# Pooled outputs of the 5x5 layer sent through DRAM and fetched back by quarters of the image

## The chip, the core and the metric

The kernel runs on one core of one Trainium2 chip. A core has TensorE (PE, matmuls, with its weight loads as PEld), VectorE (DVE), ScalarE (ACT), GpSimd (POOL) and SyncE (SP, which issues DMAs here); each takes its instructions in order, and they meet through semaphores. The metric is the device time of one execution in microseconds, the median of several runs. Less is better.

## The reference, cut to what matters

The input is 16 images of 32 channels of 128x128. Four layers follow each other, each with a group normalisation ahead of it and a residual sum behind it:

```
x = x + L0(gn(x))     a recurrent layer, 128 steps with gates
x = x + L1(gn(x))     an "adder" 3x3 layer: out = -sum |patch - w|
x = x + L2(gn(x))     a Hartley transform, 32x32 modes mixed, and back
x = x + L3(gn(x))     five edge operators, normalised, then a small U-net
```

The change lies in L3. Its first steps are

```
y = concat of five normalised 3x3 edge operators of x      (160 channels)
y = maxpool2(conv3x3(y, conv1_w) + conv1_b)                128x128 -> 64x64
y = maxpool2(conv3x3(y, conv2_w) + conv2_b)                64x64 -> 32x32
...                                                        down to 16x16 and back up
out = x * y
```

The kernel folds the edge operators, their normalisation and conv1 into one 5x5 layer of 32 input and 32 output channels, whose weights depend on the statistics of the image. As adding a constant commutes with a maximum, the bias of conv1 is added after the pooling.

## The kernel before, in words

**The stages.** stage0 computes L0. Then `rest` computes L1 with the class Differences: 16 images, two halves each, so 32 units; each unit makes 72 tiles of 128 x 64 rows x 128 or 130 columns in fp16, of |x - w| in its one-sided form, on either ScalarE (L705, `d_act`) or VectorE (L708, `d_dve`), and TensorE sums them (L595). L2 and L3 are computed by the class After for groups of four images (g = 0 to 3), 32 channels of four images filling the 128 partitions.

**The order.** All instructions are written out in one order (`keep_order` then fixes it for every engine). A planner, the class Weave, keeps planned times for PE, DVE and ACT. For each tile Differences picks the engine that would end first, at planned prices of 2.36 us for VectorE and 7.15 us for ScalarE, and between tiles `advance` lets the generator of After emit work for as long as PE has room. After's code adds its own planned prices to `weave.dve` and `weave.act`, so that the share-out of the tiles follows. `weave.later(us, step)` puts a step off by so many planned microseconds, and `weave.done(step)` runs one now if it has not run yet. Groups 0, 1 and 2 are taken one after the other beside Differences; when Differences ends, `drain` interleaves what is left of group 2 with group 3, which needs the last image; `weave.alone` is set when group 2 is done.

**The 5x5 layer** (`conv1`, L1612). The image is cut in 8 chunks of 16 rows. For each chunk, 25 taps x 16 matmuls (L1671) fill four PSUM banks, one for each image `blk` of the group. In a bank the 128 partitions are (j, o): row block j of four rows, output channel o. VectorE corrects the two border columns (L1707) and takes the 2x2 maximum into the tile `pooled` (L1595), 128 partitions of 2 rows x 64. The next layer wants another layout: tile `y1`, with partition (blk, channel) and a padded image of 66x66 in the free dimension. The helper `spread` (L1599) moves the data there: for every blk and every j it copies 32 partitions to their place and adds the bias `b1[:, blk]` on the way, on ScalarE (L1609) or, when `weave.alone` is set and blk is even, on VectorE (L1606). That is 16 small copies a chunk, put off by 5 planned us. The last chunk's `spread` is kept as `self.rest_of_y1`.

**Before and after it.** The frames of input rows come by L1307 and are normalised on ScalarE (L1313, L1319, L1320). conv2 (L1518) reads y1 in two passes of 32 rows; ahead of the second pass, `rest_of_y1` is run (L1511).

**Other transfers on SyncE.** Each unit of Differences loads its quantised image half, 2.1 MB in fp16 (`loaded`, L562, `q<-q_d`), emitted at tile 8 of the unit before; `xq` loads (L539) and their stores (L555) prepare the next image. All are issued from SyncE.

Of the kernel before, what the change touches and what calls it, by code (L numbers as in the profile page):

```python
# [7 lines left out]
F32 = mybir.dt.float32  # L8
# [897 lines left out]
class After:  # L906
# [547 lines left out]
    def first_layers(self, g, fp, frames, y2):  # L1454
        nc, tc, weave = self.nc, self.tc, self.weave
        sides = fp.tile([128, H + 4, 4], F32, name="sides")
        ops = fp.tile([128, 2, 5], F32, name="ops")
        wf = fp.tile([128, 90, 32], F32, name="wf")
        b1 = fp.tile([128, 4], F32, name="b1")
        with self.pool("e_v", self.buffers["e_v"]) as pool:  # L1460
            v = []

            def table():

                k, half = len(v) // 2, len(v) % 2
                v.append(pool.tile([128, 45, 32], F32, name="v"))
                nc.gpsimd.dma_start(
                    v[-1].rearrange("p t o -> p (t o)"), self.d["fold"][k, :, 1440 * half : 1440 * half + 1440]
                )

            with self.pool("e_s") as es:
                yield from self.statistics(g, es, frames, sides, ops, lambda: [table() for _ in range(self.buffers["e_v"])])
            yield -0.5
            for n in range(10):
                k, half = n // 2, n % 2
                for part, i in (((0, 81 - 45), 0), ((81 - 45, 45), 1)) if half else (((0, 45), 0),):
                    s = ops[:, i, k : k + 1]
                    to, t = wf[:, 45 * half + part[0] : 45 * half + part[1]], v[n][:, part[0] : part[1]]
                    if k == 0:
                        nc.vector.tensor_scalar(to, t, s, None, ALU.mult)  # L1480
                    else:
                        nc.vector.scalar_tensor_tensor(to, t, s, to, ALU.mult, ALU.add)
                    weave.dve += 0.1 + 0.033 * (part[1] - part[0])
                if len(v) < 10:
                    table()
                yield -2.0
        with self.pool("e_y1") as y1p:
            y1 = self.padded(y1p, 64, "y1")
            self.wc = {"conv2": replicated(nc, y1p, self.a["conv2"], 9, "w_conv2")}
            yield from self.conv1(g, y1p, frames, y1, sides, wf, b1)  # L1490
            with self.pool("e_c2") as cp:
                yield from self.small_layers(cp, None, y1, y2)

    def small_layers(self, cp, rp, y1, y2):
# [11 lines left out]
        def conv(src, n, name, evict):  # L1506
            rows = min(n // 4, 512 // n)
            for r in range(0, n, 4 * rows):
                acc = [self.acc() for _ in range(4)]
                if r:  # L1510
                    weave.done(self.rest_of_y1)  # L1511
                for tap in range(9):
                    kh, kw = tap // 3, tap % 3
                    for j in range(4):
                        for blk in range(4):
                            part = slice(32 * blk, 32 * blk + 32)
                            at = r + rows * j + kh
                            nc.tensor.matmul(  # L1518
                                acc[blk][32 * j : 32 * j + 32, : rows * n],
                                wc[name][part, tap, :],  # L1520
                                src[part, at : at + rows, kw : kw + n],
                                start=tap == 0,
                                stop=tap == 8,
                            )
                    yield rows * n / 512 * 1.0 + 0.15
                yield SUMMED
                for blk in range(4):
                    evict(r, rows, acc[blk][:, : rows * n], blk)
                yield -2.0
# [82 lines left out]
    def conv1(self, g, pool, frames, y1, sides, wf, b1):  # L1612
# [10 lines left out]
        ahead = self.buffers["frames"]  # L1623
        ready = {(n // 2, n % 2): normalise(n // 2, n % 2, 4.0 + 3.0 * n) for n in range(2 * ahead)}
        p = self.acc()
        for j in range(4):
            nc.tensor.matmul(p[32 * j : 32 * j + 32, :4], tap_of("all", 25), cst["m4_bc"], start=True, stop=True)
        yield SUMMED
        nc.vector.tensor_scalar(b1, p[:, :4], self.bias[:, 0:1], None, ALU.add)


        cps = [self.acc() for _ in range(4)]
# [22 lines left out]
            nc.vector.tensor_copy(cut[:, blk].rearrange("p s h r -> p (s h r)"), cps[blk][:, :64])  # L1655
        weave.dve += 0.8

        spreads = []
        for ch in range(H // R):
            xp = chunk(ch)  # L1660
            yield ("done", ready[ch, 0])
# [37 lines left out]
            if ch + ahead < H // R:  # L1699
                for half in range(2):  # L1700
                    load(ch + ahead, half)
                    ready[ch + ahead, half] = normalise(ch + ahead, half, 26.0 + 4.0 * half)
            out = []
            for blk in range(4):
                a4 = acc[blk].rearrange("p (r w) -> p r w", w=W)
                for s, col in enumerate((0, W - 1)):
                    nc.vector.tensor_tensor(a4[:, :, col], a4[:, :, col], cut[:, blk, s, ch, :], ALU.add)  # L1707
                weave.dve += 0.3
                out.append(self.pooled(pool, acc[blk], 4, W))

            def spread(top=1 + R // 2 * ch, out=out):
                for blk in range(4):
                    self.spread(
                        lambda part, j: y1[part, top + 2 * j : top + 2 * j + 2, 1:65],
                        out[blk],
                        blk,
                        b1[:, blk : blk + 1],
                        nc.scalar,
                    )

            spreads.append(weave.later(5.0, spread))
            yield -2.0
        self.rest_of_y1 = spreads.pop()
        for v in spreads:
            weave.done(v)

    def last(self, g):

# [213 lines left out]
def program(nc, tc, a, at, out):  # L1942
    def scratch(name, *shape):
        return nc.dram_tensor(name, shape, F32, kind="Internal").ap()

    d = {f"x{i}": scratch(f"x{i}_d", B, C, H, W) for i in (1, 2, 3)}
    d["q"] = nc.dram_tensor("q_d", (B, C, H + 2, W + 2), F16, kind="Internal").ap()
    d["xm"], d["z"] = (scratch(n, B, C, M1, M1) for n in ("xm_d", "z_d"))
    d["y6"] = scratch("y6_d", NG, 128, 66 * 66)
    d["fold"] = scratch("fold_d", 5, 128, 90 * 32)  # L1950
    d["up"] = scratch("up_d", 3, 128, 25 * 32)
    with tc.tile_pool(name="keep", bufs=1) as keep:
        cw = keep.tile(list(a["consts"].shape), F32, name="cw")
        nc.scalar.dma_start(cw, a["consts"])
        cst = {n: cw[:, lo:hi] for n, (lo, hi) in at.items()}
        sel16 = keep.tile([128, 9, 32], F16, name="sel16")
        nc.scalar.dma_start(sel16, a["sel16"])
        bias = keep.tile([128, 10], F32, name="bias")
        nc.scalar.dma_start(bias, a["bias"])

        m1, r1 = stage0(nc, tc, keep, cst, a["x"], a["xs"], a["w0"], a["b1"], a["b2"], d["x1"])
        rest(nc, tc, cst, sel16, bias, m1, r1, a, d, out)
# [17 lines left out]
```

## Time and profile before

| what | value |
|---|---|
| time, median of 3 runs (lowest, highest) | 7199.5 us (7186.45, 7207.52) |
| span of the profiled execution | 7206.6 us |
| busy: PE, DVE, ACT | 5631, 5845, 5498 us |
| d_act tiles on ScalarE, d_dve tiles on VectorE | 631 of 7.143 us, 1673 of 2.362 us |
| copies y<-pooled,b on ScalarE (L1609) | 488, 195.0 us, 0.400 us each |
| 5x5 layer runs (L1671): groups 0 and 1 | about 2824 to 3340 and 4470 to 4960 us, beside the adder layer |
| 5x5 layer runs: groups 2 and 3 | about 6180 to 6510 and 6680 to 7013 us, after it |
| adder layer ends | about 5945 us |
| data moved by DMA | 722.57 MB |

A line of a group gives code line, engine, operation, what is written and read, shapes and count, then busy time and mean duration, then idle time ahead of these instructions and what ended it. In a timeline, the bracket at the end of a line gives the idle time ahead of it and its releaser.

### The profile page before, as it was taken

What the parts mean: (1) busy time and instruction counts of PE and PEld (TensorE: products, weight loads), DVE (VectorE), ACT (ScalarE), POOL (GpSimd) and SP (SyncE); (2) the same over time, 40 slices, a digit from 0 to 9 for tenths busy, and PEclk for the clock granted to TensorE, in tenths of its full rate; (3) what the DMA queues carried; (4) which work ended last, traced back from release to release, by engine and by line L of the source; (5) the groups of instructions that cost most, each with busy time, mean ns of one, the idle gap of its engine ahead of it and who ended that gap; (6) DMA issues with size and microseconds to landing.
All of it is one profiled execution on the core that took longest, in us unless ns stands there. A gap on an engine that the chain in (4) does not pass through costs nothing. (4 is left out here: it accounts for less than half of the span.)

```text
span 7206.6 us, 271424 instructions
## 1 busy us (share of the span) xinstructions
PE 5631.0 (78%) x127740; PEld 3001.3 (42%) x127740; DVE 5845.3 (81%) x7099; ACT 5498.0 (76%) x3100; POOL 111.8 (2%) x91
## 2 busy tenths in 40 slices
PE   4778567777877777998777787999776784797896
PEld 3665333333334343333334343333333443554564
DVE  7787689999998989999998999999998994134224
ACT  2555489999998989999999999999998991131222
POOL 0000000000000000000000001000000000000000
PEclk9899789999988898999888998999888986798997
DMA  8664211111133432221343343221252245252324
GB/s 310 230 205 144 83 63 57 55 58 47 47 101 93 141 98 81 63 69 47 78 126 98 115 118 104 65 65 46 57 134 92 64 136 150 89 170 74 86 51 98
DMA packets 372719, 722.57 MB, mean 100 GB/s; under 512 B 50896, under 2 KB 217296, under 8 KB 360720
## 3 DMA queue, kind: packets, MB, share of 16 engines
q1 hardware_dynamic: 364128, 670.79, 30.6%
q0 software_dynamic: 7040, 33.80, 1.4%
q8 instruction: 999, 16.37, 1.0%
q14 instruction: 120, 0.98, 0.0%
q10 hardware_dynamic: 432, 0.64, 0.0%
HBM read 507.28 MB, written 164.32 MB: 93 GB/s over the span
## 5 line engine op out<-in xcount | busy, mean ns | idle before, releaser
L705 ACT ACTIVATE d_act<-q,neg 128x8192 f16<-128x8192 f16 (+1 forms) x631 | 4462.6, 7143 | 184.4 <-PE acc L595 135.0
L708 DVE TENSOR_SCALAR d_dve<-q,qw 128x8192 f16<-128x8192 f16 (+1 forms) x1673 | 3859.4, 2362 | 200.8 <-PE acc L595 158.0
L595 PE MATMUL acc<-d_dve,sel 128*32 128x512 f16 x26768 | 1869.8, 402 | 504.0 <-DVE d_dve L708 454.0
L595 PEld LDWEIGHTS <-sel 128*32 128x32 f16 x36864 | 1026.9, 100 | 2164.4 <-issue 1507.8
L1671 PE MATMUL acc<-xp,wf 32*32 32x512 f32 x25600 | 1043.7, 618 | 37.6 <-issue 32.8
L595 PE MATMUL acc<-d_act,sel 128*32 128x512 f16 x10096 | 724.4, 408 | 356.2 <-ACT d_act L705 343.6
L1671 PEld LDWEIGHTS acc<-xp,wf 32*32 32x32 f32 x25600 | 431.9, 104 | 416.5 <-issue 329.6
L625 PE MATMUL acc<-q,zero 128*32 128x512 f16 x7248 | 522.9, 401 | 0.0
L1609 ACT ACTIVATE y<-pooled,b 32x128 f32<-32x128 f32 x488 | 195.0, 400 | 414.4 <-DVE pooled L1595 407.8
L207 PE MATMUL pg<-h,wb 64*64 64x20 f32 (+15 forms) x4096 | 395.7, 320 | 106.1 <-DVE h L256 64.8
L852 PE MATMUL acc<-y,u_conv 32*32 32x256 f32 (+1 forms) x9728 | 359.8, 459 | 76.0 <-issue 46.6
L244 ACT ACTIVATE gt<-pg,bias 128x20 f32<-128x20 f32 (+15 forms) x1024 | 315.8, 374 | 80.2 <-PE pg L207 73.1
L1313 ACT ACTIVATE xp<-xp,shift,stats 128x1280 f32<-128x1280 f32 (+1 forms) x128 | 182.6, 1434 | 240.5 <-DMA xp<-x_d 210.1
L207 PE MATMUL pg<-e,wb 64*64 64x20 f32 (+15 forms) x4096 | 353.1, 315 | 16.4 <-DVE e L260 5.4
L207 PEld LDWEIGHTS pg<-h,wb 64*64 64x64 f32 x4096 | 248.3, 154 | 140.7 <-DVE h L256 90.4
L625 PEld LDWEIGHTS <-zero 128*32 128x32 f16 x7248 | 218.6, 102 | 203.0 <-issue 46.1
L207 PE MATMUL pg<-xn,wb 64*64 64x28 f32 (+61 forms) x4096 | 284.5, 302 | 11.3 <-ACT gt L244 3.8
L207 PEld LDWEIGHTS pg<-e,wb 64*64 64x64 f32 x4096 | 251.5, 156 | 92.1 <-DVE e L260 62.9
L1354 PE MATMUL acc<-xp 32*64 32x204 f32 (+3 forms) x8576 | 238.5, 344 | 37.8 <-ACT xp L1319 28.8
L1800 DVE TENSOR_SCALAR s<-acc,l_ms,l_one 128x512 f32<-128x512 f32 x128 | 102.3, 824 | 199.0 <-PE acc L852 199.0
L255 ACT ACTIVATE th<-c 128x20 f32<-128x20 f32 (+15 forms) x256 | 81.3, 320 | 235.5 <-DVE c L253 234.1
L852 PEld LDWEIGHTS acc<-y,u_conv 32*32 32x32 f32 x9728 | 171.4, 110 | 196.6 <-issue 130.4
(215 smaller groups left out, 4303.1 us busy)
## 6 DMA issues: line engine op xcount, KB each, us to landing
xr<-x_d SPq DMA_DIRECT2D x192, 512.0 KB
xp<-x_d SPq DMA_DIRECT2D x112, 640.0 KB
q<-q_d SPq DMA_DIRECT2D x32, 2145.0 KB
x_d<-xr SPq DMA_DIRECT2D x128, 512.0 KB
x_in<-in_x_dram SPq DMA_DIRECT2D x16, 2048.0 KB
res<-in_x_dram SPq DMA_DIRECT2D x64, 512.0 KB
xn<-in_xs_dram SPq DMA_DIRECT2D x64, 512.0 KB
xn<-xn SPq DMA_DIRECT2D x128, 256.0 KB
```

The source lines that it names most:

```text
L207: nc.tensor.matmul(bank[c][q][64 * pair : 64 * pair + 64, :, :width], wb[half, 4 * kind + KIND[q]].rearrange("p b o -> p (b o)"), v[half], ...
L244: nc.scalar.activation(gt[:, q, :, :n], bank[c][q][:, :, :n], AF.Tanh if q == G else AF.Sigmoid, bias=bias[:, KIND[q] : KIND[q] + 1],)
L595: self.nc.tensor.matmul(acc[k][32 * j : 32 * j + 32, :], self.sel16[:, i // 9, :], d[:, row : row + 4, c : c + W], start=first, stop=last,)
L625: self.nc.tensor.matmul(acc[k][32 * j : 32 * j + 32, :], self.zero, q[:, :4, :W], start=False, stop=False)
L705: nc.scalar.activation(dst, src, AF.Relu, bias=self.neg[:, i : i + 1])
L708: nc.vector.tensor_scalar(dst, src, self.qw[:, i : i + 1], 0.0, ALU.subtract, ALU.max)
L852: nc.tensor.matmul(acc[blk][32 * j : 32 * j + 32, o : o + rows * n], t[part, 4 * par + tap, :], src[part, top : top + rows, left : left + ...
L1313: nc.scalar.activation(v, v, AF.Identity, bias=self.shift3, scale=self.stats3[:, 1])
L1354: nc.tensor.matmul(gram[blk][j : j + width, at : at + n], xp[part, l, 2 + j : 2 + j + width], xp[part, rows, j : j + width + 4], start=sta ...
L1609: nc.scalar.activation(d, s, AF.Identity, bias=bj)
L1671: nc.tensor.matmul(acc[blk][32 * j : 32 * j + 32, :], tap_of("all", tap)[rows], xp[rows, 4 * j + kh : 4 * j + kh + 4, kw : kw + W], start= ...
L1800: nc.vector.tensor_scalar(s.rearrange("p r w b -> p b r w"), acc[blk].rearrange("p (b r w) -> p b r w", b=2, w=64), istd[:, blk : blk + 1] ...
```

## The change

The pooled outputs no longer go straight from tile to tile. VectorE writes the four maxima of a chunk into one tile `po`, and four DMAs store it at once to a DRAM buffer `y1_d`, in the layout (image, channel, pixel). At chunks 2, 4 and 6 a fetch of 16 pooled rows (two earlier chunks) into y1 is put off by 12 planned us; after the last chunk two fetches of 8 rows follow, put off by 6 and 8. With each fetch comes a step `biased`, 12 planned us later (6 for the last two), in which one ScalarE operation adds the bias in place over all 128 partitions. The bias tile therefore becomes one column over (blk, o). Before conv2 starts, the first four pieces are completed, and ahead of its second pass the last. The planner is told 0.25 + 0.054 us a row for `biased`, where it was told 0.45 us for each copy. The change is for having one ScalarE operation a quarter where there were 16 a chunk.

```diff
-        b1 = fp.tile([128, 4], F32, name="b1")
+        b1 = fp.tile([128, 1], F32, name="b1")
...
                 if r:
-                    weave.done(self.rest_of_y1)
+                    self.rest_of_y1()
...
-        for j in range(4):
-            nc.tensor.matmul(p[32 * j : 32 * j + 32, :4], tap_of("all", 25), cst["m4_bc"], start=True, stop=True)
+        for blk in range(4):
+            nc.tensor.matmul(
+                p[32 * blk : 32 * blk + 32, :1], tap_of("all", 25), cst["m4_bc"][:, blk : blk + 1], start=True, stop=True
+            )
...
-        nc.vector.tensor_scalar(b1, p[:, :4], self.bias[:, 0:1], None, ALU.add)
+        nc.vector.tensor_scalar(b1, p[:, :1], self.bias[:, 0:1], None, ALU.add)
...
-        spreads = []
+        y1_d = self.d["y1"][g]
+
+        def store(ch, po):
+            for blk in range(4):
+                to = y1_d[blk][:, 512 * ch : 512 * ch + 512]
+                first = to.offset
+                nc.sync.dma_start(
+                    bass.AP(to.tensor, first, [[128, 4], [4096, 32], [1, 128]]), po[:, blk]
+                )
+
+        coming = {}
+
+        def fetch(top, rows, after):
+            nc.sync.dma_start(
+                y1[:, 1 + top : 1 + top + rows, 1:65],
+                y1_d.rearrange("b o (r w) -> (b o) r w", w=64)[:, top : top + rows],
+            )
+            coming[top] = weave.later(after, lambda: biased(top, rows))
+
+        def biased(top, rows):
+            v = y1[:, 1 + top : 1 + top + rows, 1:65]
+            nc.scalar.activation(v, v, AF.Identity, bias=b1[:, 0:1])
+            weave.act += 0.25 + 0.054 * rows
+            coming[top] = None
+
+        def complete(top):
+            while coming.get(top):
+                weave.done(coming[top])
+
...
-            out = []
+            po = pool.tile([128, 4, 128], F32, name="po", bufs=2)
...
-                out.append(self.pooled(pool, acc[blk], 4, W))
-
-            def spread(top=1 + R // 2 * ch, out=out):
-                for blk in range(4):
-                    self.spread(
-                        lambda part, j: y1[part, top + 2 * j : top + 2 * j + 2, 1:65],
-                        out[blk],
-                        blk,
-                        b1[:, blk : blk + 1],
-                        nc.scalar,
-                    )
-
-            spreads.append(weave.later(5.0, spread))
+                src = acc[blk].rearrange("p (r a w b) -> p r w a b", a=2, b=2, w=W // 2)
+                nc.vector.tensor_reduce(po[:, blk].rearrange("p (r w) -> p r w", w=W // 2), src, AX.XY, ALU.max)
+                weave.dve += 0.65
+            store(ch, po)
+            if ch in (2, 4, 6):
+                top = 8 * ch - 16
+                coming[top] = weave.later(12.0, lambda top=top: fetch(top, 16, 12.0))
             yield -2.0
-        self.rest_of_y1 = spreads.pop()
-        for v in spreads:
-            weave.done(v)
+        coming[48] = weave.later(6.0, lambda: fetch(48, 8, 6.0))
+        coming[56] = weave.later(8.0, lambda: fetch(56, 8, 6.0))
+        for top in (0, 16, 32, 48):
+            complete(top)
+        self.rest_of_y1 = lambda: complete(56)
```

More of the change, by code (lines that the diff above doesn't have):

```diff
@@ L1948, in program @@
     d["xm"], d["z"] = (scratch(n, B, C, M1, M1) for n in ("xm_d", "z_d"))
+    d["y1"] = scratch("y1_d", NG, 4, 32, 64 * 64)
     d["y6"] = scratch("y6_d", NG, 128, 66 * 66)
```

## The prediction, made before the result was known

> **What bounds the kernel now.** I first read the page's forty slices (180 us each), to see which stages there are.
>
> ```profile
> PE   4778567777877777998777787999776784797896
> ...
> DVE  7787689999998989999998999999998994134224
> ACT  2555489999998989999999999999998991131222
> ```
>
> From slice 6 to slice 33 (900 to 5945 us) VectorE and ScalarE are both at 9 or close to it: this is the adder layer, 32 units of 72 tiles, which the two engines share out (5030 us, so 157 us a unit). After it comes a tail of 1260 us in which both are nearly idle and PE is high. Next I asked for the busy time in stretches (columns: PE, weight load, DVE, ACT, POOL, clock, DMA share, GB/s): one slice of the adder layer without the 5x5 layer, two in which the 5x5 layer (L1671) of groups 0 and 1 runs under it, then the tail in four stretches.
>
> ```profile
> 1260.00:1440.00 180.00, 137.18 (x2328) 64.26 (x2324) 177.57 (x199) 172.08 (x27) 0.00 (x0) 0.94 0.15 56
> 2880.00:3060.00 180.00, 171.92 (x3836) 64.22 (x3828) 169.51 (x112) 178.27 (x89) 0.00 (x0) 0.98 0.21 63
> 4680.00:4860.00 180.00, 178.57 (x3999) 67.36 (x3984) 173.00 (x119) 175.96 (x96) 4.68 (x1) 0.99 0.22 66
> ```
> ```profile
> 5945.00:6180.00 235.00, 105.80 (x2830) 85.93 (x2817) 98.15 (x232) 23.33 (x41) 9.06 (x14) 0.63 0.50 150
> 6180.00:6680.00 500.00, 427.44 (x13194) 246.08 (x13195) 169.11 (x454) 117.65 (x248) 8.58 (x18) 0.89 0.35 104
> 6680.00:7013.00 333.00, 302.52 (x9523) 205.00 (x9521) 80.08 (x175) 76.22 (x145) 0.21 (x1) 0.95 0.31 71
> 7013.00:7206.60 193.60, 126.09 (x4408) 84.89 (x4386) 82.81 (x171) 48.37 (x80) 0.00 (x0) 0.77 0.44 98
> ```
>
> Under the adder layer the 5x5 layer makes three engines full at once: ScalarE 178 and 176 of 180, PE 172 and 179, VectorE 170 and 173. In the tail the 5x5 layer of group 2 (6180 to 6510) and of group 3 (6680 to 7013) run on PE, with ScalarE at a quarter. So a ScalarE microsecond counts under groups 0 and 1 and is free under 2 and 3. The groups between 2880 and 3240 us show what this ScalarE time is made of (count, busy us, mean ns, idle before):
>
> ```profile
> L705 ACT ACTIVATE d_act<-q,neg 128x8192 f16<-128x8192 f16 (+1 forms) x42 | 297.9, 7146 | 1.9 <-PE acc L595 1.7
> ...
> L1609 ACT ACTIVATE y<-pooled,b 32x128 f32<-32x128 f32 x96 | 38.3, 399 | 1.3
> ...
> L543 ACT ACTIVATE xq<-xq,shift,r 128x1024 f32<-128x1024 f32 x4 | 4.9, 1232 | 1.6 <-DMA xq<-x_d 1.6
> ```
>
> The 96 small bias copies take 38 us of 360 and wait for almost nothing; a copy of 128x1024 takes 1.23 us. Last I looked for what a late transfer does in this layer, in the timelines of SyncE, ScalarE and VectorE around 2550 to 2605 us:
>
> ```profile
> 2549.65 0.56 SPq L562 DMA_DIRECT2D q<-q_d  x1
> 2557.11 37.98 SPq L1307 DMA_DIRECT2D xp<-x_d  x3
> ```
> ```profile
> 2596.48 1.46 ACT L1313 ACTIVATE xp<-xp,shift,stats 128x1280 f32<-128x1280 f32 x1 [23.29 <-DMA xp<-x_d]
> ```
> ```profile
> 2601.86 2.35 DVE L708 TENSOR_SCALAR d_dve<-q,qw 128x8192 f16<-128x8192 f16 x1 [17.79 <-PE acc L595]
> ```
>
> A frame load queued behind the 2.1 MB load of q came late, ScalarE stood 23.3 us, and PE and VectorE followed: 17.8 us lost by all. A transfer that ScalarE waits for in its in-order queue is no private matter of ScalarE.
>
> **What the Trainium skill says.** (1) "DMA: Bandwidth & Descriptors", section "Why a DMA increments its semaphore by 16 and not by 1": a transfer is spread over the largest number of engines up to 16 that divides the slowest dimension of both sides. The load of q starts with a broadcast dimension of 4, hence 4 engines; the trace agrees, with a DMA share of 0.25 to 0.28 for some 35 us after its issue at 4490.7. The new stores also start with a dimension of 4, and the fetches with 128. (2) Same page, "Queues, rings and completion order": each engine takes one issuer's descriptors in ring order. So a fetch on 16 engines has a quarter of its pieces behind a running q load; the two waits above agree, and so does the xq load issued at 3030.5, for which ScalarE waited until 3071. (3) Same page, "Anatomy of one DMA — SWDGE (gpsimd) path": about 2 us fixed, most of it the receipt of the write. That is told of the other issue path; the chain here shows a 640 KB frame load at 4.7 us. (4) Same page, "Why small descriptors are slow (HBM only)": 256-byte pieces cost 27% more; the fetches' rows are 64 x 4 = 256 bytes. No row of before shows that.
>
> **The change, part by part.**
> Removed from ScalarE, per group: 8 chunks x 16 copies x 0.400 = 51.2 us. Added: three of 16 rows (128x1024, 1.23 us) and two of 8 rows (128x512, not shown; on the line between 0.40 at 128 elements and 1.23 at 1024 it is 0.76): 5.2 us. Net 46 us a group, 92 us in the two groups under the adder layer. There the planner gives x tiles from VectorE (2.36 us each) to ScalarE (7.14): 2.36x = 92 - 7.14x, x = 9.7, and both end **23 us** earlier. The planner's own prices (0.45 a copy, 0.25 + 0.054 a row) free 105.8 us, 11.1 tiles, 26 us. I take 23, bounds 15 and 27.
>
> Unchanged: eight border additions and four reductions a chunk on VectorE; the four matmuls of the bias (one column for four). The 32 stores and 5 fetches a group take SyncE about 0.5 us each (L555, 0.54 us), 20 us a group, on a queue with some 20 issues in 360 us: nothing. The stores wait for the four reductions, some 4 us after the chunk's last matmul; queued behind them are frame, xq and q loads issued 10 us and more ahead of their use: nothing to 2 us. Traffic: 4 MB a group on 722 MB.
>
> Added wait: a ScalarE bias op for each fetch, planned 12 us after it (6 for the last two). A fetch lands in about 6 us (4.7 us for 640 KB, 512 KB with the 27%, and its issue); behind q it takes up to 40 (3030.5 to 3071). The slack is 12 us plus half a tile of ScalarE queue, 16, less 6: 10 us. The q load fills 35 of 157 us, so of ten fetches under the adder layer about 2 fall into it, and such a one is on average (35-10)^2/(2 x 35) = 9 us too late. Of that the buffers hide some 5 (23.3 against 17.8). Expected **5 to 8 us**, bounds 0 and 40; I take 5.
>
> Moved: PE. With 46 us of ScalarE free, 6.4 more tiles are made while one group's 5x5 layer runs, each about 1.1 us of PE (L595: 232 us for 224 tiles, and L610), and PE was full: 7 us, and the tiles made in those 7 us again, 7/(1-0.54) = 15 us a group. So at the end of the adder layer, 23 us sooner, group 2 stands 23 + 30 = 53 us further back. Its missing work there (end of the Hartley back transform, 7 us an iteration that holds 1.3 us of PE) shrinks to about 25 us once nothing paces it; and in the tail it then waited for transfers anyway (ScalarE 25.6, 11.2 and 14.9 us for frames between 5940 and 5996). PE fills only from 6180. I take **5 us** of lengthening, bounds 0 and 25.
>
> The junction to conv2 in the tail: the 5x5 layer ended at 7012.9, conv2's first pass ran at once until 7023.4, the last copy began at 7018.2. Now: reductions until 7017, store 2 to 3 us, fetch 4 to 6, bias 0.8: 7024 to 7027. The second pass waits 1 to 4 us; I take **2**. In group 2 ScalarE stands in this wait with group 3's frames behind it: 0 to 5, counted in the 5 above.
>
> Sum: 7199.5 - 23 + 5 + 5 + 2 = 7188 (7188.5).
>
> **Rivals.**
> (B) Full gain: no fetch meets a q load, and group 2's delay vanishes in the transfers of 5945 to 6180, where PE is 45% busy: 7199.5 - 26 - 4 (less contention on ScalarE in the tail) = 7170. For it: those transfer waits; against it: two frame or xq loads did meet q in before.
> (C) The gain is paid back: two late fetches at 9 and the whole 7 us of (A)'s rest: 7199.5 - 23 + 18 + 7 = 7202, no change. For it: ScalarE's 23 us stall that carried VectorE along.
> (D) Slower: the late fetches hit the quarter before conv2, where PE itself stands in its in-order queue, so with two full hits at 18 us and group 2's 25 us, 7199.5 - 23 + 36 + 25 = 7238. For it: in before the q load of 3318 would still run when the last eighth of group 0 is stored (after 3337); PE is full from 6180, so lateness of group 2 can come through whole. Against it: both bounds at once.
>
> **How the numbers follow.** A 0.42 (7188, give or take 15: 0.13 faster by over 0.3%, that is below 7178; 0.26 within; 0.03 slower). B 0.23 (0.22 faster, 0.01 within). C 0.14 (0.09 within, 0.05 slower, above 7221). D 0.21 (slower). Together faster 0.35, same 0.36, slower 0.29. The range 7150 to 7240 leaves out the outer half of D and the best of B. The planner lays the whole order anew, and no row of before shows how its chunks fall against the q loads; that is the greatest unknown.
>
> **What would show it.** Right: ScalarE's copies y<-pooled,b gone, ten bias ops of about 1.2 and 0.8 us under the adder layer; L705's count up by about 10 and L708's down by as many; the adder layer's last d_dve near 5922 instead of 5944; the tail 1262 to 1275 us. Wrong: ScalarE idle behind a DMA into y1 by more than 15 us in all, with VectorE idle on PE of like length; the first L1671 of group 2 more than 260 us after the adder layer's end; PE idle ahead of conv2 (L1518) by over 5 us in group 3. The forecast fails upwards if fetches are late more than twice, downwards if the tail shortens too.

## The result, and the profile after

The changed kernel takes 7370.5 us (median of 4 runs, 7358.3 to 7371.8) against 7202.3 us for the kernel before (7186.5 to 7207.5): a ratio of 1.0235, interval 1.0219 to 1.0250. It is 168 us slower, above the forecast range.

The loss has two seats. The adder layer ends at 6016 us instead of 5941.5 (+75), and the tail behind it lasts 1354 us instead of 1265 (+88). The page's forty slices of the changed kernel, now 184 us each:

```profile
PE   4788477778777778887776776988877776599986
...
DVE  7787599999989989887998998988999892512334
ACT  2556399999989999888998999988999860120101
```

ScalarE and VectorE fall to 8, in one slice to 7, in slices 17 to 19 and 27 to 28, counted from 1, while the 5x5 layer (now L1701) of groups 0 and 1 runs: the stretches where both were full. The same stretches in numbers, as shown for before, then the tail in four parts (columns: PE, weight load, DVE, ACT, POOL, clock, DMA share, GB/s):

```profile
1260.00:1440.00 180.00, 137.14 (x2348) 64.54 (x2344) 177.57 (x200) 173.27 (x27) 0.00 (x0) 0.95 0.15 55
2880.00:3060.00 180.00, 167.30 (x3648) 62.72 (x3618) 167.94 (x112) 158.47 (x35) 0.00 (x0) 0.96 0.25 67
4680.00:4860.00 180.00, 170.60 (x3852) 65.37 (x3841) 173.00 (x111) 174.99 (x40) 0.00 (x0) 0.98 0.21 65
```
```profile
6016.00:6430.00 414.00, 249.19 (x5612) 200.37 (x5611) 199.86 (x470) 48.44 (x89) 18.08 (x31) 0.61 0.66 207
6430.00:6700.00 270.00, 241.90 (x7285) 141.83 (x7284) 65.19 (x174) 48.82 (x82) 2.59 (x6) 0.91 0.31 86
6700.00:7112.00 412.00, 373.01 (x12276) 268.26 (x12276) 104.09 (x294) 46.04 (x63) 0.42 (x2) 0.97 0.25 58
7112.00:7369.00 257.00, 174.72 (x5658) 107.39 (x5654) 113.33 (x225) 39.19 (x41) 0.00 (x0) 0.76 0.48 106
```

The stretch at 1260 is as before. At 2880, ScalarE has 35 instructions instead of 89, is 20 us less busy, and PE lost 4.6 us with it: the relief is there, and time is lost beside it. In the tail, the stretch up to group 2's 5x5 layer (PE busy 249 of 414 us, clock 0.61) is longer: the layer's first L1701 starts 420 us after the adder layer's end. In before the first L1671 of group 2 starts at 6204.8 us, 263 us after the end, and not at 6180, where the stretches above the prediction put it.

What holds ScalarE in the adder layer is said by its waits (us in total, times, longest), in before from 2700 us to 5941 us and in after from 2700 us to 6016 us:

```profile
ACT d_act L705 <- PE acc L595: 109.0, 26, 14.3
ACT xp L1313 <- DMA xp<-x_d: 1.9, 1, 1.9
```
```profile
ACT y L1681 <- DMA y<-y_d: 136.6, 7, 28.5
ACT d_act L705 <- PE acc L595: 104.6, 27, 19.7
ACT xp L1313 <- DMA xp<-x_d: 23.2, 3, 18.3
```

The bias operation (L1681) stands 136.6 us behind its fetch, in 7 waits for its ten fetches. Five waits, of 21 to 29 us, belong to the six large fetches (16 rows) and make 123 us of the sum. The other two, of 8.3 and 5.2 us, come at the end of each group's layer, where the last stores, a fetch of 8 rows and its bias follow each other directly. The first of the five, in the timelines of SyncE, ScalarE and VectorE:

```profile
3027.26 2.40 SPq L1666 DMA_DIRECT2D y_d<-po  x3
3029.76 0.65 SPq L562 DMA_DIRECT2D q<-q_d  x1
3030.46 0.83 SPq L1673 DMA_DIRECT2D y<-y_d  x1
```
```profile
3064.78 1.15 ACT L1681 ACTIVATE y<-y,b 128x1024 f32<-128x1024 f32 x1 [24.15 <-DMA y<-y_d]
3065.84 1.45 ACT L1313 ACTIVATE xp<-xp,shift,stats 128x1280 f32<-128x1280 f32 x1
```
```profile
3079.99 4.62 DVE L708 TENSOR_SCALAR d_dve<-q,qw 128x8192 f16<-128x8192 f16 x2 [22.11 <-PE acc L595]
```

The fetch is issued 0.7 us after the load of q and lands some 34 us later; ScalarE stands 24 us, and VectorE stands 22 us until 3080, because PE had waited 22.7 us for ScalarE's tile. It is the picture shown for a frame load of before, but it repeats. In group 0 the loads of q are issued at 3029.8, 3180.8 and 3344.4 us and the fetches at 3030.5, 3182.7 and 3348.9; in group 1 two of three again follow within 3 us (4869.5 and 4871.3; 5033.3 and 5035.8), and the third fetch leaves 8 us ahead of its load (5188.3 and 5196.4) and isn't waited for. Five of six is hard to put down to chance. A fetch comes every second chunk, and group 0's 5x5 layer now holds 285 tiles, so 285/4 = 71 tiles from fetch to fetch; a load of q comes every 72 tiles. The two periods are nearly equal, so one meeting is followed by the next. With the 251 tiles of before it would be 63 tiles, and in e6 below, which has that share-out, two of six follow a load of q directly. This reading rests on issue times; no run varied the period alone.

The share-out moved, but little of it the way it was meant to (first two lines of before, then of after):

```profile
L705 ACT ACTIVATE d_act<-q,neg 128x8192 f16<-128x8192 f16 (+1 forms) x631 | 4462.6, 7143 | 184.4 <-PE acc L595 135.0
L708 DVE TENSOR_SCALAR d_dve<-q,qw 128x8192 f16<-128x8192 f16 (+1 forms) x1673 | 3859.4, 2362 | 200.8 <-PE acc L595 158.0
```
```profile
L705 ACT ACTIVATE d_act<-q,neg 128x8192 f16<-128x8192 f16 (+1 forms) x637 | 4505.5, 7146 | 177.6 <-PE acc L595 128.0
L708 DVE TENSOR_SCALAR d_dve<-q,qw 128x8192 f16<-128x8192 f16 (+1 forms) x1667 | 3844.9, 2361 | 304.8 <-PE acc L595 261.3
```

Six tiles went from VectorE to ScalarE, and VectorE's wait for PE grew by 103 us (158.0 to 261.3). What moved more is the place of the tiles. Between the first and the last L1671 or L1701, group 0 had 251 tiles and has 285, group 1 251 and 282; behind group 1's 5x5 layer 403 were left and now 329. So less of the adder layer is left for group 2 to hide in, and its 5x5 layer starts 157 us later after the adder layer's end, at 420 us instead of 263. There it falls together with group 3's (matmuls of the layer in four stretches, counted from the adder layer's end, of before and of after):

```profile
5941.00:6191.00 250.00, 0.00 (x0) 0.62 0.51 150
6191.00:6541.00 350.00, 257.47 (x6400) 0.96 0.38 116
6541.00:6891.00 350.00, 162.61 (x3221) 0.85 0.33 81
6891.00:7206.00 315.00, 113.90 (x3190) 0.86 0.33 74
```
```profile
6016.00:6266.00 250.00, 0.00 (x0) 0.58 0.65 203
6266.00:6616.00 350.00, 115.70 (x3056) 0.80 0.47 142
6616.00:6966.00 350.00, 287.06 (x7498) 0.97 0.22 60
6966.00:7370.00 404.00, 98.26 (x2286) 0.82 0.44 96
```

The stretch from 600 us after the end on has 6411 of some 12,800 matmuls in before and 9784 in after.

### The profile page after: what moved, and what is told of

Same layout as the page of the kernel before. It is cut to its first block, busy times and chain, and to the rows that moved or that the text cites. A ratio compares the mean times of both kernels' runs of the same rounds, so it can differ in the third digit from the quotient of the medians.

```text
span 7370.0 us, 270488 instructions
## 1 busy us (share of the span) xinstructions
PE 5654.5 (77%) x127400; PEld 3063.2 (42%) x127400; DVE 5833.6 (79%) x7109; ACT 5353.7 (73%) x2598; POOL 108.4 (1%) x91
## 5 line engine op out<-in xcount | busy, mean ns | idle before, releaser
L705 ACT ACTIVATE d_act<-q,neg 128x8192 f16<-128x8192 f16 (+1 forms) x637 | 4505.5, 7146 | 177.6 <-PE acc L595 128.0
L708 DVE TENSOR_SCALAR d_dve<-q,qw 128x8192 f16<-128x8192 f16 (+1 forms) x1667 | 3844.9, 2361 | 304.8 <-PE acc L595 261.3
L595 PE MATMUL acc<-d_act,sel 128*32 128x512 f16 x10192 | 748.6, 416 | 504.4 <-ACT d_act L705 494.3
L1701 PE MATMUL acc<-xp,wf 32*32 32x512 f32 x25600 | 994.3, 614 | 29.3 <-issue 17.8
L1701 PEld LDWEIGHTS acc<-xp,wf 32*32 32x32 f32 x25600 | 425.7, 104 | 365.6 <-issue 288.7
L625 PE MATMUL acc<-q,zero 128*32 128x512 f16 x6908 | 497.8, 399 | 0.0
L1354 PE MATMUL acc<-xp 32*64 32x204 f32 (+3 forms) x8576 | 257.0, 357 | 82.5 <-ACT xp L1319 64.2
L1354 PEld LDWEIGHTS acc<-xp 32*64 32x64 f32 (+1 forms) x8576 | 176.3, 140 | 177.1 <-issue 103.3
L207 PEld LDWEIGHTS pg<-xn,wb 64*64 64x64 f32 x4096 | 220.8, 156 | 35.7 <-ACT gt L244 8.2
```

The lines of the kernel that those rows point to most:

```text
L207: nc.tensor.matmul(bank[c][q][64 * pair : 64 * pair + 64, :, :width], wb[half, 4 * kind + KIND[q]].rearrange("p b o -> p (b o)"), v[half], ...
L595: self.nc.tensor.matmul(acc[k][32 * j : 32 * j + 32, :], self.sel16[:, i // 9, :], d[:, row : row + 4, c : c + W], start=first, stop=last,)
L625: self.nc.tensor.matmul(acc[k][32 * j : 32 * j + 32, :], self.zero, q[:, :4, :W], start=False, stop=False)
L705: nc.scalar.activation(dst, src, AF.Relu, bias=self.neg[:, i : i + 1])
L708: nc.vector.tensor_scalar(dst, src, self.qw[:, i : i + 1], 0.0, ALU.subtract, ALU.max)
L1354: nc.tensor.matmul(gram[blk][j : j + width, at : at + n], xp[part, l, 2 + j : 2 + j + width], xp[part, rows, j : j + width + 4], start=sta ...
```

## The experiments

Three explanations were set against each other: the fetches come late and stop ScalarE (theory 1, "ring", in the expectations); the share-out puts more tiles on a full PE and pushes group 2 into the tail (theories 2 and 4); the traffic through DRAM and SyncE's waits cost the time by themselves (theory 3). Below, "lead" is the time from the end of group 1's 5x5 layer to the adder layer's end. Before ran at 7204.7, 7209.2, 7215.0 and 7215.0 us beside the four sets of runs (e1 to e4, e5 to e8, e9 to e11, e12 and e13); each ratio is to the one beside it. Adder layer, tail and waits are of the profiled execution of each run.

**e1: the fetch issued by ScalarE.** L1673 in the changed kernel, nothing else:

```diff
-            nc.sync.dma_start(
+            nc.scalar.dma_start(
                 y1[:, 1 + top : 1 + top + rows, 1:65],
```


> The kernel after, with its 20 fetches of y1 issued from ScalarE's queue instead of SyncE's; nothing else moves, the order on PE and VectorE is the same. Theory 1 (ring): a fetch issued from SyncE stands behind the 2.1 MB load of q on the four DMA engines that this load uses, ScalarE stands in its bias op until then, and PE and VectorE follow; from another issuer's ring the fetch is taken in turn. Then ScalarE's waits on y1 under the adder layer fall from 128 us to under 30, the adder layer ends by 5950 us (6016 now), and the time is 7170 to 7260 us. Theory 2 (PE): the 5x5 layer takes longer because a freed ScalarE makes more tiles for a full PE, and group 2 slides into the tail whatever the fetches do: 7330 to 7375 us. Theory 3 (SyncE): the stores' waits on VectorE hold up the loads behind them on SyncE: 7330 to 7375 us.

Measured: 7279.1 us, ratio 1.0097 (1.0082 to 1.0112), 91 us less than the changed kernel, but 19 us above the range of theory 1. L1681 waits 4.5 us instead of 136.6 before the adder layer's end, which comes at 5902; the tail stays at 1376, so late fetches are not the tail's cause.

The fetches are not only in another queue here, they also leave earlier. SyncE had four stores that wait for VectorE, and the load of q, ahead of the fetch in its order; ScalarE had not:

```profile
3012.14 0.39 ACTq L1673 DMA_DIRECT2D y<-y_d  x1
```
```profile
3023.06 7.44 SPq L1666 DMA_DIRECT2D y_d<-po  x4
3030.60 0.65 SPq L562 DMA_DIRECT2D q<-q_d  x1
```

All six large fetches leave 2.5 to 18.5 us ahead of the load of q, and by the trace's DMA packets each had landed before the first packet of that load moved. So e1 shows that the place behind q costs the time. It does not show that a fetch from another issuer's queue passes a load of q that is already running; e5 has one that didn't.

**e2, e3: the load of q on all engines,** in the changed kernel and in the kernel before:

```diff
-        self.nc.sync.dma_start(q, bass.AP(q_d.tensor, first, [[0, 4], [(H + 2) * P, C], [1, (self.R + 2) * P]]))
+        for k in range(4):
+            self.nc.sync.dma_start(
+                q[32 * k : 32 * k + 32].rearrange("p r w -> p (r w)"),
+                bass.AP(q_d.tensor, first, [[(H + 2) * P, C], [1, (self.R + 2) * P]]),
+            )
```


> The kernel after, with the load of q written as four loads of 32 partitions, so that each is spread over 16 DMA engines and not 4. Theory 1 (ring): q is through in some 10 us instead of 35, fetches are not late any more, ScalarE's waits on y1 under the adder layer fall under 30 us, 7150 to 7230 us. Theory 2 (PE): 7330 to 7375 us, as PE's work is the same. Theory 3 (SyncE): 7330 to 7375 us, and three more issues per unit on SyncE.

> The kernel before with the same split of the load of q. Theory 1 (ring): before had two stalls of 23 us behind q; without them 7150 to 7190 us. Theories 2 and 3: no change, 7190 to 7210 us.

Measured: e2 7203.0 us, 1.0000 (0.9991 to 1.0009); e3 7169.4 us, 0.9945 (0.9929 to 0.9962). The split is worth 167 us to the changed kernel and 35 to the kernel before, so 132 of the 168 us need the slow load of q. But e2 is still 34 us behind e3, and its bias operation (there L1685) still waits 73.3 us (7 times, longest 17.9), where under 30 was expected: five of the six large fetches follow q as before, and the load of q is through in 23.6 us from its first issue (median) and not in the 10 expected, against 36.9 in the changed kernel. The adder layer of e2 ends at 5834 (e3: 5907), its tail is 1367 (e3: 1266).

In e3 the time is as expected, but not by the two stalls named alone: 22 of its 35 us are won at the head of the adder layer, where the first tile waits for the first load of q and starts at 897 us instead of 920. The stall of a frame load of 23.3 us is gone; the one of an xq load stays (21.2 us). The split load alone, which could have been made in the kernel before, beats both kernels.

**e4: the relief alone.** In the kernel before, one ScalarE operation a chunk from the weights tile in place of 16 copies, no transfers. It leaves out the pooled outputs:

```diff
-                for blk in range(4):
-                    self.spread(
...
+                src = wf[:, :16, :].rearrange("p t o -> p (t o)").rearrange("p (r w) -> p r w", w=64)
+                nc.scalar.activation(y1[:, top : top + 8, 1:65], src, AF.Identity, bias=b1[:, 0:1])
+                weave.act += 0.25 + 0.054 * 8
```


> The kernel before, in which ScalarE's 16 copies of pooled outputs a chunk are replaced by one operation of 128x512 from the weights tile, so that y1 holds no pooled data (left out: the layout change of the pooled outputs); no stores and no fetches. It is the relief of ScalarE without the way through DRAM. Theory 1 (ring): the forecast gain of 23 us appears, 7165 to 7190 us. Theory 2 (PE): the relief itself does the harm, 7280 to 7375 us. Theory 3 (SyncE): like theory 1, 7165 to 7190 us.

Measured: 7190.2 us, 0.9977 (0.9967 to 0.9987), 14.5 us less than before and at the upper edge of the range of theory 1. Eleven tiles moved to ScalarE (642 of L705, 1662 of L708), as the balance has it, but the adder layer ended at 5944, no sooner. From 900 us to there ScalarE waited 53 us for frames and 152 us for PE (before: 25 and 135): 45 us of its relief turned into waits. The gain lies in the tail, 1244 us against 1265. So with this load of q even a bounce through DRAM that cost nothing would hardly have brought the 23 us where they were forecast.

**e5, e6: the old share-out.** e1, and e2, with the planner told 7.2 us of ScalarE a chunk, as for the copies, and nothing for the bias operations:

```diff
             store(ch, po)
+            def charge():
+                weave.act += 7.2
+            weave.later(5.0, charge)
```


> The kernel with fetches from ScalarE's queue, in which the planner is charged what the removed copies cost (7.2 us of ScalarE per chunk, 5 us after it) and nothing for the bias ops, so that it shares out the tiles as in the kernel before; the work is that of the kernel after. Theory 4 (share-out): the planner turns ScalarE's freed time into more tiles while the 5x5 layer runs, PE is full, the layer spans 285 and 282 tiles instead of 251, group 2 starts late and slides into the tail. Then with the old charge the layer spans about 251 tiles, group 2's statistics begin before the adder layer ends, the tail is about 1260 us and not 1377, and the time is 7180 to 7215 us. If the slide comes from the way through DRAM itself: 7260 to 7285 us as with fetches from ScalarE alone.

> The kernel after with the load of q split over 16 DMA engines and the planner charged as before. Theory 4 (share-out): no slide, so as the kernel before with the split, 7160 to 7190 us. If what was left between these two (34 us) is the bias ops' wait for ordinary fetches: 7195 to 7215 us.

Measured: e5 7245.1 us, 1.0046 (1.0031 to 1.0061); e6 7190.5 us, 0.9973 (0.9961 to 0.9985). The tiles are back where they were (251 or 252 under each 5x5 layer; 402 and 403 left), and so is group 2: its 5x5 layer starts 262 and 261 us after the adder layer's end, and the tail is 1281 and 1280. So the long tail is the share-out's. But the adder layer ends later, by 59 us against e1 and 70 us against e2, and the net is 34 and 12.5 us only (4 to 5 us more when each run is taken against the before beside it). So e5 lies above its range of 7180 to 7215 us, and e6 at the upper edge of its own. What stays against the kernel with the same q load and share-out is 36 us (e5 to before) and 21 us (e6 to e3); 16 and 14 of it lie in the tail. In e5, 19 lie in the adder layer, where ScalarE waits 33.1 us for fetches and 11.7 us for stores that its own queue of issues now has to wait for. One of these fetches, of 8 rows, leaves ScalarE's queue while a load of q is running (issues on SyncE and ScalarE, then the bias operation):

```profile
3320.14 1.33 SPq L562 DMA_DIRECT2D q<-q_d  x1
```
```profile
3337.04 0.37 ACTq L1673 DMA_DIRECT2D y<-y_d  x1
```
```profile
3360.81 0.72 ACT L1681 ACTIVATE y<-y,b 128x512 f32<-128x512 f32 x1 [14.72 <-DMA y<-y_d]
```

By the trace's DMA packets, 768 of its 1024 pieces of 256 bytes have started by 3341 us, within 3 us of the first. From 3341 to 3355 only 81 more do, beside 83 pieces of q, and the last one lands at 3360.4, after q's last at 3359.0. This agrees with the Trainium skill, "DMA: Bandwidth & Descriptors", section "Queues, rings and completion order": SyncE and ScalarE each own a ring on each of the same DMA engines, and an engine takes turns between rings packet by packet. Taking turns with pieces of q of 17 KB, the quarter of the fetch that shares q's engines came as late as q itself. The trace doesn't say which engine took which piece, so this last step is a reading.

**e7: the bias later.** The changed kernel, with `biased` of the first three quarters planned 40 us after its fetch instead of 12:

```diff
-                coming[top] = weave.later(12.0, lambda top=top: fetch(top, 16, 12.0))
+                coming[top] = weave.later(12.0, lambda top=top: fetch(top, 16, 40.0))
```


> The kernel after, all DMAs on SyncE, but the bias ops of the first three quarters planned 40 us after their fetch instead of 12. Theory 1 (ring): the fetches are as late as before, but ScalarE doesn't stand there for them; the adder layer ends at 5895 to 5930 us and the time is 7265 to 7300 us (the slide into the tail stays). If the harm is done by late loads behind the stores on SyncE: 7340 to 7375 us.

Measured: 7270.5 us, 1.0085 (1.0070 to 1.0100), 100 us less than the changed kernel. L1681 waits 17.5 us. The fetches still queue behind q; only nobody stands waiting for them. The 17.5 us are the two waits at the ends of the layers (8.4 and 9.1). With e1 this settles the first half: what costs is ScalarE's place in its in-order queue, not the lateness of the data. The tail is 1363: untouched.

**e8: the traffic alone.** The kernel before in full, and added to it the stores, and fetches of equal size and time from that buffer into a DRAM buffer that nobody reads:

```diff
+                nc.sync.dma_start(
+                    bass.AP(to.tensor, to.offset, [[128, 4], [4096, 32], [1, 128]]),
...
+                weave.later(12.0, lambda top=8 * ch - 16: fetch(top, 16))
```


> The kernel before, in full, plus the stores of the pooled outputs and fetches of the same size and rhythm, which go from the DRAM buffer to another DRAM buffer that nobody reads. It has the transfers and SyncE's waits without the waits of ScalarE and without a new share-out. Theories 1 and 4: 7195 to 7225 us. Theory 3 (SyncE's waits and traffic): 7280 us or more.

Measured: 7259.7 us, 1.0066 (1.0049 to 1.0083), 50 us more than before: the adder layer 5947 (+5), the tail 1307 (+42). In the adder layer the traffic costs next to nothing when ScalarE doesn't wait for it. In the tail, where the DMA share is highest, it does cost. The time lies between the ranges of the theories. Its fetches also write to DRAM, which those of the change don't, and e5 and e6 have tails only 16 and 14 us longer, with the real traffic, its bias operations and its waits together: e8 probably overstates the traffic.

**e9: the share-out alone.** The kernel before with q split; the planner is told a wrong price for each copy:

```diff
-                weave.act += 0.45
+                weave.act += 0.04
```


> The kernel before with the split load of q, in which the planner is told 0.04 us instead of 0.45 for each of ScalarE's small copies y<-pooled,b (and the like ones of the later layers). All copies, and nothing else, are as before: no transfer, no bias operation is added. So the planner believes in the same relief that the change gave, and the relief is not there. If the longer tail of the changed kernel comes from the share-out (the planner lays more tiles beside the 5x5 layer of groups 0 and 1, group 2 is pushed back), this kernel shows 275 to 290 tiles in each of the two 5x5 layers instead of 252, under 345 tiles left after the second, the 5x5 layer of group 2 starting over 380 us after the adder layer's end (263 with the split load), and a tail of 1330 to 1380 us against 1266; time 7240 to 7290. If the transfers through DRAM make the longer tail, the tail stays below 1285 us and the time within 7165 to 7200.

Measured: 7206.7 us, 0.9986 (0.9977 to 0.9995). 265 and 282 tiles, 371 left, the start of group 2's 5x5 layer at 297 us, a tail of 1278. Neither expectation was met: group 0 took 13 more tiles than e3 instead of some 30, the tail grew by 13 us only, and the time, which lies between the two ranges, is lost in the adder layer (5939 us, e3: 5907). Either the share-out was not the tail's cause, or its effect is a step that this run doesn't reach.

**e10, e11: PE's work let further ahead,** in e2 and in e3:

```diff
-SLACK, CLOCK = 3.0, 1.0
+SLACK, CLOCK = 6.0, 1.0
```


> The changed kernel with the split load of q, in which the planner lets PE's work of the groups run 6 us ahead of the next tile instead of 3 (SLACK 3.0 to 6.0). If the tail is long because the work of group 2 is pushed back, letting it in sooner shortens the tail: more than 345 tiles left after the second 5x5 layer (329 without), the 5x5 layer of group 2 starting under 390 us after the adder layer's end, a tail under 1340 us (1367 without), at the price of some waits of the tiles on PE, adder layer 0 to 20 us later; time 7165 to 7205. If the planner is held by something else than this bound, nothing changes by over 10 us: 7193 to 7213.

> The kernel before with the split load of q and the same larger bound (6 us instead of 3). By the same theory the tail is shorter than 1266 us, by 0 to 40, and the adder layer later by 0 to 25: 7150 to 7185 against 7169 with the split load alone. By the rival nothing changes by over 10 us.

Measured: e10 7272.9 us, 1.0085 (1.0063 to 1.0108); e11 7223.2 us, 1.0009 (1.0001 to 1.0017). Both miss by far, upwards. The tail shrinks to 926 and 844 us, the adder layer stretches to 6348 and 6377. Work moved out of the tail comes back in the adder layer with a surcharge: 421 us of tail less, 470 of adder layer more in e11. That is why the place of group 2 alone says so little about the total.

**e12, e13: group 2 as far back as in the change, without its transfers.** As e9, but by -0.8 us a copy; and by `SLACK` 2.0, with ScalarE's share planned truly:

```diff
-                weave.act += 0.45
+                weave.act += -0.8
```
```diff
-SLACK, CLOCK = 3.0, 1.0
+SLACK, CLOCK = 2.0, 1.0
```


> The kernel before with the split load of q, in which the planner is told -0.8 us instead of 0.45 for each of ScalarE's small copies; all copies, and nothing else, are as before. It is made so that in the planner's own time the stretch from the end of group 1's 5x5 layer to the end of the adder layer is as short as in the changed kernel (712 planned us against 711; 892 in the kernel before, 838 in the run with 0.04). If the place of group 2 makes the tail, with a step at the point where its Hartley back transform no longer fits before the adder layer's end, then this stretch measures about 745 us, group 2's back transform (L1267) begins after the adder layer's end, its 5x5 layer starts over 390 us after it, and the tail is 1335 to 1375 us. If the transfers through DRAM are needed for the long tail, the tail stays below 1300 us. The adder layer may end anywhere, since ScalarE is given more than it can do.

> The kernel before with the split load of q, in which the planner lets PE's work of the groups run only 2 us ahead of the next tile instead of 3. ScalarE's share is planned truly; PE's work of the groups is held back by the other means (677 planned us from the end of group 1's 5x5 layer to the adder layer's end, against 892). If the place of group 2 makes the tail, whatever put it there, the tail is 1340 us or more and the adder layer ends sooner than 5907 us, at 5830 to 5880: 7180 to 7240 together. If what counts is the mispriced ScalarE or the transfers, the tail stays below 1300 us.

Measured: e12 7280.2 us, 1.0086 (1.0070 to 1.0103): 330 tiles left, lead 771 us, start at 414 us, tail 1340, within the range of the first theory. e13 7166.4 us, 0.9931 (0.9916 to 0.9945): 309 tiles left, lead 712, start at 414, tail 1361, also as that theory had it; the adder layer is over at 5804, sooner than expected, and so the time is below its range. The second half is settled by these: no pooled output goes through DRAM in them, and the tail is as long as after. The runs with `SLACK` 2.0 or 3.0 stand in two lots:

| run | lead, us | group 2's 5x5 starts after the end | tail, us |
|---|---|---|---|
| before, e3 | 956, 933 | 263, 263 | 1265, 1266 |
| e5, e6 | 967, 940 | 262, 261 | 1281, 1280 |
| e9, e4 | 875, 819 | 297, 284 | 1278, 1244 |
| e12, after, e1 | 771, 765, 762 | 414, 420, 429 | 1340, 1354, 1376 |
| e7, e2, e13 | 757, 742, 712 | 412, 426, 414 | 1363, 1367, 1361 |

Only e8, with traffic of its own, stands between them (lead 957, start at 263, tail 1307). Between a lead of 819 and one of 771 us the tail steps by 60 to 100 us. What changes there is seen in the matmuls of the Hartley back transform, in e9, in e12 and in the changed kernel, in the last 250 us of the adder layer and in the two stretches of 250 us after it (busy us, count, clock, DMA share, GB/s):

```profile
5689.00:5939.00 250.00, 18.38 (x256) 0.92 0.35 108
5939.00:6189.00 250.00, 0.00 (x0) 0.66 0.53 154
6189.00:6439.00 250.00, 19.31 (x256) 0.86 0.42 127
```
```profile
5691.00:5941.00 250.00, 3.59 (x54) 0.92 0.23 70
5941.00:6191.00 250.00, 28.73 (x202) 0.60 0.64 196
6191.00:6441.00 250.00, 47.21 (x256) 0.70 0.49 155
```
```profile
5766.00:6016.00 250.00, 0.00 (x0) 0.88 0.23 71
6016.00:6266.00 250.00, 40.22 (x256) 0.58 0.65 203
6266.00:6516.00 250.00, 40.72 (x256) 0.73 0.51 159
```

With a long lead, group 2's 256 matmuls are done before the adder layer ends. With a short one they fall wholly (after) or for the most part (e12: 202 of 256, where the expectation had all of them) into the transfer-laden start of the tail, at 196 to 203 GB/s and a clock of 0.58 to 0.60, and there they keep PE busy for up to twice the time (40 us for 256 in after instead of 18 in e9). That the place of group 2 makes the tail is shown by e12 and e13; that this transform is what makes it a step is read from the trace and wasn't tried by itself. Nor is it shown where the last 20 of group 0's 34 extra tiles come from: the lower price alone brought 13 or 14 (e4 and e9 both have 265).

e13 also says what a late group 2 costs by itself: against e3 the adder layer is 103 us shorter and the tail 96 us longer, so next to nothing in the total. It and e3 are the fastest kernels here, and no different from each other by their intervals.

## Why the prediction was wrong, point by point

- **What bounds the kernel** was read rightly: three engines full under groups 0 and 1. The conclusion from it failed in part. ScalarE's freed time wasn't worth its length: the tiles moved in e4 (11, where 9.7 were forecast), but the 23 us did not come in the adder layer (+3 us there, a gain of 14.5 us in the whole), while ScalarE waited 28 us longer for frames and 17 us longer for PE.
- **Added wait, taken as 5 us: the first step that failed.** The mechanism was the one described (a fetch behind q, ScalarE in its queue, PE and VectorE after it). Its size was off by a factor of nearly twenty: 91 us (e1) to 100 us (e7), outside the bounds of 0 and 40. The count of hits was taken from chance, 35 of 157 us, so 2 of 10. Five of the six large fetches were hit, as both streams are paced by the same tiles, 71 and 72 of them. The size of a hit was taken as an average over chance places in the load, 9 us. But SyncE issues the fetch 0.7 to 4.5 us behind q, so each hit met nearly the whole load, and the wait was 25 us on average, the prediction's own 35 - 10. The waits at the end of the layer, 8.3 and 5.2 us, were priced in the tail alone, and hiding the waits was assumed from one example. The sign that the prediction set for itself, fetches late more than twice, came true.
- **Moved: PE, taken as 5 us: the second.** 15 us a group were forecast; the tiles under the layer grew by 34 and 31, and even without the late fetches each layer is 49 us longer (e1: 560.8 and 559.0 against 511.7 and 509.6). Group 2 was to be 53 us further back at the end, but its lead fell by 191. "It waited for transfers anyway" failed: group 2's 5x5 layer starts 157 us later after the end, and the tail is 88 us longer. On the other side of the same move, the adder layer is shorter for it (59 us, e5 to e1), which the forecast left out too. Net it is 34 us (e1 to e5), or 12.5 (e2 to e6). The start of group 2's layer was also misread: the sign "more than 260 us after the adder layer's end" is met by before itself (263 us).
- **The junction to conv2, taken as 2 us,** was about right for group 3: PE waits 3.9 us in e6, where 1 to 4 were given. Its timeline has

```profile
6995.40 5.55 PE L1522 MATMUL acc<-y,w_conv 32*32 32x512 f32 x82 [3.93 <-ACT y L1685]
```

  The last store was issued at 6986.0 at the latest, the fetch at 6991.4, the bias operation began at 6994.6: at most 5.4 us for the store where 2 to 3 were taken, 3.2 for the fetch where 4 to 6 were.
- **Durations** were right: 1.15 us and 0.72 us for the two bias shapes (1.23 and 0.76 taken). So was the landing of a large fetch with nothing in its way: 4.0 to 5.0 us from issue to last packet for five of six in e1 (6 taken). The prediction's 27% for 256-byte pieces was misread: in the Trainium skill, "DMA: Bandwidth & Descriptors", section "Why small descriptors are slow (HBM only)", it is the share of overhead in the whole. No run here shows it.
- **"Nothing" for stores and traffic** holds in the adder layer (e8: +5 us), not in the tail: e5 and e6 are 16 and 14 us longer there, with the bias operations' waits among them.
- **Sum.** From before to after by the runs: 36 us that stay with early fetches and the old share-out (e5 to the before beside it), 34 for the share-out (e1 to e5), 91 for the fetches behind q (after to e1), 161 of 168. The missing 7 are the difference between the two befores, 7209.2 and 7202.3. Rival D named both terms, at 36 and 25 us, though it laid the late fetches just ahead of conv2, where the two waits were the short ones. The prediction held "both bounds at once" against it. The runs suggest that the share-out feeds both, since five of six large fetches follow q with the new one (e2) and two of six with the old one (e6); the old share-out with the unsplit load and the fetches on SyncE was not run.

## What to carry to other kernels

When a consumer in an in-order queue is tied to a transfer, look at what stands ahead of that transfer in its issuer's queue, and whether both are paced by the same loop; if they are, count them as meeting nearly always or nearly never, not by chance, and at the place that the queue's order gives. Put the wait far behind the issue, or have the fetch leave ahead of the large load, before asking for the gain. And where a planner fills a freed engine, ask which other engine's work it pulls forward with it: here ScalarE's freed time became tiles laid beside a PE that was full, and the work they pushed out came back in the tail.

## What the runs showed of the hardware

- What counts is whether a fetch leaves ahead of a large load or behind it. Large fetches that left 0.7 to 4.5 us behind the load of q on SyncE were waited for 21 to 29 us each (changed kernel); those that left 2.5 to 18.5 us ahead of it weren't waited for (e1). The one that left ScalarE's queue 17 us behind it was waited for 14.7 us (e5): the other queue was no protection.
- The load of q, with its leading broadcast dimension of 4, took 36.9 us from issue to last packet in before (median). As four loads by partitions it takes 25.8 us, and the kernel before is 35 us faster (e3): 22 of them at the first load, which the adder layer waits for. ScalarE's waits for frames in the adder layer shrink from 25.1 to 12.4 us.
- A store to DRAM and a fetch of it back took at most 5.4 and 3.2 us in a quiet stretch, from issue to issue and from issue to use (e6).
